# A convolution's first image: the table stored unnormalised, its scale and mean put back later

## The chip, the cores and the metric

The kernel runs on one core of one Trainium2 chip. The metric is the time of the device in microseconds for one execution. The engines are called PE (TensorE), DVE (VectorE), ACT (ScalarE), POOL (GpSimd) and SP (SyncE).

## The reference

The input `x` has 4 images of 256 channels and 64 x 64 positions. Layer 0 is a deformable convolution of the normalised images, added to `x`; layer 1 is an attention between the images and a mixture of experts. The change lies in layer 0 alone, and there in the first image alone:

```python
def _gn(v, G=32, eps=1e-5):            # mean and variance over 8 channels and all positions
    g = v.reshape(B_, G, C_ // G, H_, W_)
    ...
    return ((g - m) / jnp.sqrt(s + eps)).reshape(v.shape)

om = conv(x, w_off) + b_off            # x is the normalised image; 27 values a position
off = om[:, :2 * K2]                   # offsets of the 9 taps
mask = sigmoid(om[:, 2 * K2:])         # one factor for each tap and position
...
sampled = bilinear(x, ys, xs)          # 4 corners, weighted; outside the image: 0
sampled = sampled * mask
out = einsum('bckhw,ock->bohw', sampled, w_conv)
```

## The kernel before

An image is held channel by channel: two halves (`NCH` = 2, index `ch`) of 128 channels on the partitions, 4096 positions along them. Eight blocks (`NBLK`, index `q`) of 512 positions (`BLK`) make an image, and four groups (`NT`, index `i`) of 128 positions make a block.

**The opening** prepares the first image before any gather. SP issues the load of the image in four pieces (`load_piece`, L363), then the weights of the offsets (`woff_sb`, L376), `boff_sb` (L382), the weights of the convolution (`wconv_sb`, L394) and the zeros around the table (`borders`, L404 to L408). DVE takes the statistics of each piece as it comes (`stats`, L446); a small chain over PE, DVE and POOL gives for each channel the group's mean `gm`, the scale `rs` and the shift `nb` = -`gm` x `rs` (`group_of` to `shift`, L452 to L475). Then each block is normalised on DVE (`norm`, L508), turned by PE so that positions lie on the partitions (`turn`, L517), copied out of PSUM by ACT, and for the last group by DVE (`leave`, L530), and stored to the table in DRAM by four DMAs (L536). A row of the table holds the 256 channels of a position and those of the position below it; two rows, one after the other, are the four corners of a bilinear sample. The tiles that a turned block is collected in are `gs`, the ten buffers (`NGB`) that the gathers use afterwards. After that the offsets of the first two blocks (`EARLY`) are made: six products a block into `po` (`rows_of`, L548), three shifted copies by ACT into `oc` (L560), sums over the taps (`summed`, L569), and from them the indices and weights (`positions`, L626 to L648).

**The loop** then makes 288 steps (`STEPS`) for each image, one for every 128 positions and tap `k`. In iteration `n`: POOL gathers four corners for a later step (`gather`, L748; a buffer is used again when DVE has read its last corner); ACT weighs the first corner (`corner0`, L772, four steps ahead); DVE adds the other three (`corner`, L781); PE turns the sum back to channels (`turned`, L795) into one of three PSUM buffers of `ps_tp`; ACT copies the turned tile of the step before to `sT` (`to_sbuf`, L803); and PE makes one of the four products of an earlier tap (`product`, L815), which add up over the taps in `acc`. Work for the next image (load, statistics, table, offsets) and the offsets of the first image's other blocks are strung into the same loop at written-out steps: `later.append((step, fn))`.

The order on PE, DVE, ACT and POOL is the written one, in the opening (`emit(first)`, without POOL) as in the loop; an instruction that waits holds up all that follow it on its engine. SP issues its DMAs in the order in which they are written, or when their data are ready.

Of the kernel before, what the change touches and what calls it, by code (L numbers as in the profile page):

```python
# [9 lines left out]
F32 = mybir.dt.float32  # L10
I32 = mybir.dt.int32
AF = mybir.ActivationFunctionType
ALU = mybir.AluOpType
# [4 lines left out]
P = 128  # L18
B, C, H, W = 4, 256, 64, 64
HW = H * W  # L20
NCH = C // P
K2 = 9
NR = HW // P
NOFF = 3 * K2
QUAD = 32
# [10 lines left out]
BLK = 512  # L36
NT = BLK // P
RB = BLK // W


STEPS = NR * K2
# [4 lines left out]
OUT = 6  # L46
EARLIEST = 12
FIRST = 32
LOADS = (8, 18, 28, 38)
LANDED = 7  # L50
FIRST_HALF, SECOND_HALF = 189, 58
# [4 lines left out]
NBLK = HW // BLK  # L56
# [46 lines left out]
def conv_attn_moe_kernel(  # L103
# [229 lines left out]
    with ExitStack() as actx:  # L333
# [6 lines left out]


        azt = made.enter_context(tc.tile_pool(name="a_zt", bufs=2, side="right"))
        apad = made.enter_context(tc.tile_pool(name="a_pad", bufs=2, side="right"))
        atmp = made.enter_context(tc.tile_pool(name="a_tmp", bufs=1, side="right"))
        axs = [
# [14 lines left out]
        def load_piece(b, n):  # L360
            ch, h = divmod(n, 2)
            cols = slice(h * HW // 2, (h + 1) * HW // 2)
            return nc.sync.dma_start(  # L363
                xraw[b][:, ch, cols],
                x[b, ch * P : (ch + 1) * P].rearrange("p h w -> p (h w)")[:, cols],
            )

        image_tile(0)
        for n in range(2 * NCH):
            load_piece(0, n)  # L370


        woff_sb = aw.tile([P, NCH, 3, 3, QUAD], F32, name="woff_sb")
        V.memset(woff_sb, 0.0)
        for ch in range(NCH):
            nc.sync.dma_start(  # L376
# [9 lines left out]
            V.tensor_copy(tap_sum[ps], ident[ps, kj * QUAD : kj * QUAD + NOFF])  # L386


        ocs = [aw.tile([3 * QUAD, RB, W], F32, name=f"oc{n}") for n in range(3)]
# [3 lines left out]
        for ch in range(NCH):  # L393
            nc.sync.dma_start(wconv_sb[:, ch], w_conv[ch * P : (ch + 1) * P])  # L394
        rwc_sb = load_router(aw, "rwc_sb")


        zeros = aw.tile([P, C], F32, name="zeros")
        G.memset(zeros, 0.0)

        def borders(b):
# [6 lines left out]
            nc.sync.dma_start(  # L408
                tables[b].rearrange("(y x) (two c) -> y (x two) c", x=TW, two=2)[
                    : H + 1, 2 * (W + 1) :  # L410
                ],
                zv[: H + 1].to_broadcast([H + 1, 4, C]),
            )


        grid = aw.tile([P, 2, NR, K2], F32, name="grid")
# [14 lines left out]
        def pieces(b):  # L431
# [28 lines left out]
            def shift():  # L460
                V.scalar_tensor_tensor(nb, gm, -1.0, rs, ALU.mult, ALU.mult)

            n = FIRST
            out_ = later if b else first
            for ch in range(NCH):
                for j in range(NBLK):
                    at = LOADS[2 * ch + 2 * j // NBLK] + LANDED + j % (NBLK // 2)
                    out_.append((at if b else n, lambda ch=ch, j=j: stats(ch, j)))
                    n += 1
# [10 lines left out]
            xrv = xr.rearrange("p ch (h w) -> p ch h w", w=W)  # L480
            tv = tables[b].rearrange("(y x) (two c) -> y x two c", x=TW, two=2)
            oms = []

            def block(q, at, table=True, offsets=True, alone=False):

# [35 lines left out]

                def leave(i):
                    if i == 0:

                        t["zt"] = (
                            gs[q].rearrange("p (t c) -> p t c", c=C) if alone
                            else azt.tile([P, NT, C], F32, name=f"zt{b}_{q}", tag="zt")
                        )
                    zt = t["zt"]
                    (V.tensor_copy if alone and i == NT - 1 else S.copy)(zt[:, i, :], t["tp"])  # L530
                    if i < NT - 1:
                        return
                    for yl in range(2):
                        for two in range(2):
                            yy = q * RB + yl + 1 - two
                            stores[b] = nc.sync.dma_start(  # L536
                                tv[yy : yy + RB - 1 : 2, 1 : W + 1, two, :].rearrange(
                                    "t x c -> x t c"
                                ),
                                zt[yl * W : (yl + 1) * W],  # L540
                            )


                def rows_of(n):
# [6 lines left out]
                        start=(n == 0), stop=(n == NCH * 3 - 1),  # L551
                    )

                oc = ocs[q % 2 if table else 2]

                def shifted(kj):
                    ps = slice(kj * QUAD, (kj + 1) * QUAD)
# [6 lines left out]
                def summed(half):  # L564
# [3 lines left out]
                    for i in range(half * 2, half * 2 + 2):  # L568
# [2 lines left out]
                            start=True, stop=True,  # L571
                        )

                def kept():
                    if b and not q:
                        oms.append(atmp.tile([P, NR, NOFF], F32, name=f"om{b}", tag="om"))
                    of[q] = oms[0][:, rows_in(q), :] if b else atmp.tile(
                        [P, NT, NOFF], F32, name=f"om{b}_{q}", tag="om_", bufs=2
                    )
                    V.tensor_copy(of[q], t["pt"])  # L580

                out_.append((at, lambda: norm(0)))
                out_.append((at + 1, lambda: norm(1)))
                if alone and table:
                    for i in range(NT):
                        out_.append((at + 10 + 2 * i, lambda i=i: turn(i)))
                        out_.append((at + 11 + 2 * i, lambda i=i: leave(i)))
                elif table:
                    for i in range(NT):
                        out_.append((at + 3 + 4 * i, lambda i=i: turn(i)))  # L590
                        out_.append((at + 4 + 4 * i, lambda i=i: leave(i)))
                if offsets:
                    for m in range(NCH * 3):
                        out_.append((at + 4 + 2 * m + m // 2, lambda m=m: rows_of(m)))
                    for kj in range(3):
                        out_.append((at + 18 + kj, lambda kj=kj: shifted(kj)))
                    out_.append((at + 22, lambda: summed(0)))
                    out_.append((at + 23, lambda: summed(1)))
                    out_.append((at + 24, kept))
                return out_  # L600

            of = {}
# [105 lines left out]


            place_for()  # L710
            for q in range(NBLK):
                first.extend(block(q, n + 10 * q, offsets=False, alone=True))
            n += 10 * NBLK + 8
            for q in range(EARLY):
                at = n + 20 * q
                first.extend(block(q, at, table=False, alone=True))
# [82 lines left out]
        def to_sbuf(n):  # L799
            tap, i = divmod(n, NT)  # L800
            if i == 0:
                sTs[tap] = asm.tile([P, NCH, BLK], F32, name=f"sT{tap}", tag="sT", bufs=2)
            S.copy(  # L803
                sTs[tap][:, :, i * P : (i + 1) * P],
                tps.pop(n).rearrange("p (ch t) -> p ch t", ch=NCH),
            )

        def product(n):

            tap, part = divmod(n, NT)  # L810
            block, k = divmod(tap, K2)
            oh, ch = divmod(part, NCH)
            if k == 0 and ch == 0:
                accs[block, oh] = ps_acc.tile([P, BLK], F32, name=f"acc{block}_{oh}", tag="acc")
            T.matmul(  # L815
                accs[block, oh], wconv_sb[:, ch, k, oh * P : (oh + 1) * P], sTs[tap][:, ch, :],
                start=(k == 0 and ch == 0), stop=(k == K2 - 1 and ch == NCH - 1),
            )
            if part == NT - 1:
                del sTs[tap]  # L820

# [1331 lines left out]
```

## Time and profile before

| | us |
|---|---|
| median of 3 runs | 2981.97 (2981.52 to 2986.56) |
| the profiled execution | 2980.43 |
| its span in the profile | 2978.6 |
| first gather issued | 62.70 |
| PE busy over the span | 2808.4 (94%) |
| DVE, ACT, POOL busy | 2460.5 (83%), 1897.9 (64%), 1767.1 (59%) |

The shares of busy time are averages over stages with different limits. What matters here is the opening, up to the first gather, and the loop over the first image, up to about 510 us. A matmul's duration in a row includes the filling of the array; the distance from one start to the next is what it costs where PE is full. "x2" in a timeline counts instructions that stand side by side.

### The profile page before, as it was taken

To read this page: it belongs to the slowest core of one execution; us is meant where nothing else is said; L and a number is where in the kernel's file an instruction comes from. 1 tells how busy PE (TensorE), PEld (TensorE's weight loads), DVE (VectorE), ACT (ScalarE), POOL (GpSimd) and SP (SyncE) were. 2 spreads that over 40 slices of the span, in tenths; PEclk is the share of its full clock that TensorE was granted. 3 is DMA by queue.
4 is the path that set the end of the run, shared out by engine and by line. 5 is a ranking of instruction groups with operands and counts; after the bars stand their busy time and mean duration, and the time that the engine had idled before them with its cause. 6 is when DMAs were issued, how large, how long until landed. Compare 5 with 4: busy or idle time off the path is not lost. (4 is left out here: it accounts for less than half of the span.)

```text
span 2978.6 us, 46093 instructions
## 1 busy us (share of the span) xinstructions
PE 2808.4 (94%) x11356; PEld 1650.3 (55%) x11356; DVE 2460.5 (83%) x6413; ACT 1897.9 (64%) x4462; POOL 1767.1 (59%) x1809
## 2 busy tenths in 40 slices
PE   3899999899998899999999999999999999999997
PEld 2355554345554455544444444545555688888885
DVE  4988889998999999999999996987778785446777
ACT  2566665566765566755776664764876666666675
POOL 2665556666666676667777663320777677774442
PEclk8999999999999999999999999999999999999998
DMA  8999999999999999999999986961555556647988
GB/s 256 409 352 368 350 350 403 406 389 399 410 391 401 406 393 400 402 393 389 408 395 382 383 339 139 177 108 55 189 176 197 184 171 195 207 146 248 339 278 280
DMA packets 348551, 913.03 MB, mean 307 GB/s; under 512 B 42566, under 2 KB 125821, under 8 KB 345984
## 3 DMA queue, kind: packets, MB, share of 16 engines
q0 software_dynamic: 208368, 689.10, 62.5%
q1 hardware_dynamic: 129488, 197.93, 20.9%
q10 hardware_dynamic: 10432, 23.07, 2.1%
q8 instruction: 95, 1.56, 0.2%
q14 instruction: 168, 1.38, 0.1%
HBM read 741.09 MB, written 171.60 MB: 306 GB/s over the span
## 5 line engine op out<-in xcount | busy, mean ns | idle before, releaser
L748 POOL DMA_INDIRECT g<-table,idx x1152 | 1119.2, 971 | 611.7 <-DVE s L781 526.5
L815 PE MATMUL acc<-sT,wconv_sb 128*128 128x512 f32 x2304 | 1186.8, 597 | 22.3 <-ACT sT L803 18.8
L772 ACT ACTIVATE s<-g,wts 128x256 f32<-128x256 f32 x1152 | 587.0, 510 | 316.0 <-DMA g<-table,idx 241.3
L781 DVE SCALAR_TENSOR_TENSOR partial<-g,wts,s 128x256 f32<-128x256 f32 x1152 | 565.3, 491 | 124.2 <-ACT s L772 48.0
L795 PEld LDWEIGHTS tps<-ident,s 128*128 128x128 f32 x2304 | 295.3, 147 | 659.6 <-issue 275.1
L781 DVE SCALAR_TENSOR_TENSOR s<-g,wts,s 128x256 f32<-128x256 f32 x1152 | 550.1, 478 | 0.0
L803 ACT COPY sT<-tps 128x256 f32<-128x256 f32 x1152 | 417.8, 363 | 204.9 <-PE acc L815 113.6
L781 DVE SCALAR_TENSOR_TENSOR s<-g,wts,partial 128x256 f32<-128x256 f32 x1152 | 545.2, 473 | 0.7
L795 PE MATMUL tps<-ident,s 128*128 128x128 f32 x2304 | 458.6, 281 | 84.9 <-DVE s L781 43.7
L1935 POOL DMA_INDIRECT ys_rows<-y,to x277 | 276.0, 996 | 221.6 <-DVE y L1930 162.8
L815 PEld LDWEIGHTS acc<-sT,wconv_sb 128*128 128x128 f32 x2304 | 349.4, 192 | 33.2 <-ACT sT L803 30.5
L1508 POOL DMA_INDIRECT xs_rows<-u,slots x256 | 253.4, 990 | 95.0 <-issue 69.7
L1907 PE MATMUL ph<-xT,w 128*128 128x256 f32 (+1 forms) x1288 | 268.6, 351 | 7.4 <-ACT hT L1911 4.5
L1925 PE MATMUL py<-w,hT 128*128 128x256 f32 x1108 | 266.5, 380 | 0.6 <-ACT w L1874 0.6
L1930 DVE TENSOR_TENSOR y<-py,w 128x512 f32<-128x512 f32 (+1 forms) x161 | 99.3, 617 | 188.0 <-ACT w L1868 94.0
L1907 PEld LDWEIGHTS ph<-xT,w 128*128 128x128 f32 x1288 | 210.9, 191 | 28.6 <-ACT hT L1911 6.9
L1925 PEld LDWEIGHTS py<-w,hT 128*128 128x128 f32 x1108 | 206.9, 190 | 27.4 <-ACT w L1874 1.0
L1911 ACT ACTIVATE hT<-ph,w 128x256 f32<-128x256 f32 (+1 forms) x322 | 136.8, 443 | 129.1 <-PE ph L1907 127.5
L322 DVE SCALAR_TENSOR_TENSOR junk<-q,k 128x512 f32<-128x512 f32 x224 | 141.6, 686 | 20.6 <-ACT k L1107 20.5
L548 PE MATMUL po<-xs,woff_sb 128*96 128x512 f32 x288 | 147.2, 593 | 0.0
L1290 DVE SCALAR_TENSOR_TENSOR mix<-pv,att,mix 128x512 f32<-128x512 f32 x192 | 132.6, 742 | 6.8 <-PE pv L1026 2.8
L1874 ACT COPY w<-early_state 128x768 f32 x161 | 132.8, 825 | 0.0
(291 smaller groups left out, 3434.5 us busy)
## 6 DMA issues: line engine op xcount, KB each, us to landing
xt<-xs_rows SPq DMA_DIRECT2D x116, 260.0 KB
yk<-ys_rows SPq DMA_DIRECT2D x56, 512.0 KB
table<-zt SPq DMA_DIRECT2D x96, 256.0 KB
g<-table,idx POOLq DMA_INDIRECT x1152, 7.7
t<-o SPq DMA_DIRECT2D x32, 530.0 KB
t<-bo_sb POOLq DMA_DIRECT2D x32, 530.0 KB, 15.2
dt<-t SPq DMA_DIRECT2D x64, 265.0 KB
xraw<-in_x SPq DMA_DIRECT2D x16, 1024.0 KB
```

The lines of the kernel that those rows point to most:

```text
L322: V.scalar_tensor_tensor(junk, qks[s_, j, ch][0], 1.0, qks[t_, j, ch][1], ALU.mult, ALU.mult, accum_out=parts[:, ch, s_ * B + t_, j : j + 1],)
L548: T.matmul(t["po"], woff_sb[:, ch, ki].rearrange("p kj o -> p (kj o)"), t["xs"][:, ch, ki : ki + RB], start=(n == 0), stop=(n == NCH * 3 - 1),
L748: g = G.indirect_dma_start(out=gs[n % NGB], out_offset=None, in_=tables[b], in_offset=bass.IndirectOffsetOnAxis(ap=params[b][0][:, r, k : ...
L772: first = S.activation(ss[n], gs[n % NGB][:, :C], AF.Copy, scale=params[b][1][:, 0, r, k : k + 1])
L781: last_corner[n] = V.scalar_tensor_tensor(kept if c == 1 else ss[n], gs[n % NGB][:, c * C : (c + 1) * C], params[b][1][:, c, r, k : k + 1] ...
L795: T.transpose(tps[n][:, ch * P : (ch + 1) * P], s[:, ch * P : (ch + 1) * P], ident)
L803: S.copy(sTs[tap][:, :, i * P : (i + 1) * P], tps.pop(n).rearrange("p (ch t) -> p ch t", ch=NCH),)
L815: T.matmul(accs[block, oh], wconv_sb[:, ch, k, oh * P : (oh + 1) * P], sTs[tap][:, ch, :], start=(k == 0 and ch == 0), stop=(k == K2 - 1 a ...
L1508: s = G.indirect_dma_start(out=rows_, out_offset=bass.IndirectOffsetOnAxis(ap=slots[:, k, n : n + 1], axis=0), in_=u[:, n % NT, :], in_off ...
L1907: T.matmul(ph, w1_sb[:, ch, f * P : (f + 1) * P], xT[:, ch, :], start=(ch == 0), stop=(ch == NCH - 1),)
L1925: T.matmul(py[:, i, :], hT[:, f, i * P : (i + 1) * P], w2_sb[:, f, :], start=(f == 0), stop=(f == NCH - 1),)
L1935: s = G.indirect_dma_start(out=ys_rows[g], out_offset=bass.IndirectOffsetOnAxis(ap=to[:, i : i + 1], axis=0), in_=y[:, i, :], in_offset=No ...
```

## The change

Only the first image is treated differently. Its groups of 128 positions are turned straight from the loaded image (`raw`), as soon as the first halves of both channel halves are there, and stored without scale and mean; for that the four pieces of the load are issued in another order. The first 24 groups (`RAW`) come before the chain of the statistics on PE and ACT, the other 8 after it. As a place outside the image must count as zero after the normalisation, the border of the table now holds the mean of each channel (`mean_row`), so its stores come after the statistics; and the loads of `wconv_sb` and `rwc_sb` come after all stores of the table.

In the loop, the scale of each channel is applied where the turned tile is copied to `sT`: two ACTIVATEs of 128x128 with a scale for each partition take the place of one copy of 128x256. The mean is taken out by a product: `centre` (9 x 256) is the shift `nb` multiplied into the convolution's weights, made by `centre_part` at steps 1 to 5 of the loop, and each block's `acc` gets one more product for each half of its output, of `centre` with the masks of the nine taps. These are made by `turned_mask`, one product and one sigmoid for each block. The tile `spare`, in which the mean's row and `centre` are put together, takes the place that the second image is loaded to.

```diff
         image_tile(0)
-        for n in range(2 * NCH):
-            load_piece(0, n)
+        for h in range(2):
+            for ch in range(NCH):
+                load_piece(0, 2 * ch + h)
...
+            def raw(q, i):
+                zt = gs[q].rearrange("p (t c) -> p t c", c=C)
+                tp = ps_tp.tile([P, C], F32, name=f"tpx{b}_{q}_{i}", tag="tp")
+                for ch in range(NCH):
+                    T.transpose(
+                        tp[:, ch * P : (ch + 1) * P],
+                        xr[:, ch, q * BLK + i * P : q * BLK + (i + 1) * P], ident,
+                    )
+                S.copy(zt[:, i, :], tp)
+                if i == NT - 1:
+                    stored(q, zt)
+
+            def mean_row():
+                scale_of[b] = rs
+                pr = ps_om.tile([P, C], F32, name="mean_row", tag="om")
+                for ch in range(NCH):
+                    d = spare[:, 0, ch * P : (ch + 1) * P]
+                    V.tensor_scalar(d, ident, gm[:, ch : ch + 1], None, ALU.mult)
+                    T.matmul(pr[:, ch * P : (ch + 1) * P], ones, d, start=True, stop=True)
+                row = spare[:, 0, C : 2 * C]
+                S.copy(row, pr)
+                borders(b, row)
+
+            def centre_part(m):
+                ks = slice(2 * m, min(2 * m + 2, K2))
+                size = (ks.stop - ks.start) * C
+                pc = ps_tp.tile([1, BLK], F32, name=f"pc{m}", tag="tp")
+                for ch in range(NCH):
+                    T.matmul(
+                        pc[:, :size], nb[:, ch : ch + 1],
+                        wconv_sb[:, ch, ks].rearrange("p k o -> p (k o)"),
+                        start=(ch == 0), stop=(ch == NCH - 1),
+                    )
+                S.copy(spare[:1, 1, 2 * m * C : 2 * m * C + size], pc[:, :size])
+                if ks.stop == K2:
+                    nc.sync.dma_start(
+                        centre, spare[:1, 1, : K2 * C].rearrange("p (k o) -> p k o", o=C)
+                    )
...
-                oc = ocs[q % 2 if table else 2]
+                oc = ocs[0 if table else 1]
...
+                def turned_mask():
+                    pk = ps_tp.tile([K2, BLK], F32, name=f"pk{q}", tag="tp")
+                    T.matmul(
+                        pk, tap_sum[:, 2 * K2 :], oc.rearrange("p y x -> p (y x)"),
+                        start=True, stop=True,
+                    )
+                    masks[q] = asm.tile([K2, BLK], F32, name=f"mT{q}", tag="mT", bufs=2)
+                    S.activation(masks[q], pk, AF.Sigmoid)
...
                     out_.append((at + 24, kept))
+                    if not b:
+                        out_.append((at + 24, turned_mask))
...
-            for q in range(NBLK):
-                first.extend(block(q, n + 10 * q, offsets=False, alone=True))
-            n += 10 * NBLK + 8
+            for m in range(NBLK * NT):
+                q, i = divmod(m, NT)
+                at = 2 * q // NBLK if m < RAW else n + (m - RAW) / 2
+                first.append((at, lambda q=q, i=i: raw(q, i)))
+            first.append((n, mean_row))
+            n += 8
+            for m in range((K2 + 1) // 2):
+                later.append((1 + m, lambda m=m: centre_part(m)))
...
-            S.copy(
-                sTs[tap][:, :, i * P : (i + 1) * P],
-                tps.pop(n).rearrange("p (ch t) -> p ch t", ch=NCH),
-            )
+            tp = tps.pop(n).rearrange("p (ch t) -> p ch t", ch=NCH)
+            to = sTs[tap][:, :, i * P : (i + 1) * P]
+            if n >= STEPS:
+                S.copy(to, tp)
+                return
+            for ch in range(NCH):
+                S.activation(
+                    to[:, ch], tp[:, ch], AF.Copy, scale=scale_of[0][:, ch : ch + 1]
+                )
...
+            if block < NBLK and k == 1 and ch == 1:
+                T.matmul(
+                    accs[block, oh], centre[:, oh * P : (oh + 1) * P], masks[block],
+                    start=False, stop=False,
+                )
...
-        borders(0)
         todo = {}
         for when, fn in pieces(0):
             todo.setdefault(when, []).append(fn)
+        for ch in range(NCH):
+            nc.sync.dma_start(wconv_sb[:, ch], w_conv[ch * P : (ch + 1) * P])
+        rwc_sb = load_router(aw, "rwc_sb")
```

Left out are tiles moved to other pools, `stored` (the four stores of a block, unchanged, now a function) and the branches of `leave` and `block` that only the first image's table used.

More of the change, by code (lines that the diff above doesn't have):

```diff
@@ L48 @@
 FIRST = 32
+RAW = 24
 LOADS = (8, 18, 28, 38)
@@ L342, in conv_attn_moe_kernel @@
         azt = made.enter_context(tc.tile_pool(name="a_zt", bufs=2, side="right"))
+        amade = made.enter_context(tc.tile_pool(name="a_made", bufs=1, side="right"))
         apad = made.enter_context(tc.tile_pool(name="a_pad", bufs=2, side="right"))
@@ L368, in conv_attn_moe_kernel @@
         image_tile(0)
-        for n in range(2 * NCH):
-            load_piece(0, n)
-        woff_sb = aw.tile([P, NCH, 3, 3, QUAD], F32, name="woff_sb")
+        for h in range(2):
+            for ch in range(NCH):
+                load_piece(0, 2 * ch + h)
+        woff_sb = amade.tile([P, NCH, 3, 3, QUAD], F32, name="woff_sb")
         V.memset(woff_sb, 0.0)
@@ L386, in conv_attn_moe_kernel @@
             V.tensor_copy(tap_sum[ps], ident[ps, kj * QUAD : kj * QUAD + NOFF])
-        ocs = [aw.tile([3 * QUAD, RB, W], F32, name=f"oc{n}") for n in range(3)]
+        ocs = [amade.tile([3 * QUAD, RB, W], F32, name=f"oc{n}") for n in range(2)]
         for oc in ocs:
@@ L392, in conv_attn_moe_kernel, with borders @@
         wconv_sb = aw.tile([P, NCH, K2, C], F32, name="wconv_sb")
[L393 to L398, printed above, removed]
+        centre = aw.tile([K2, C], F32, name="centre")
+        spare = axs[1].tile([P, NCH, HW], F32, name="spare", tag="xraw")
+        masks, scale_of = {}, {}
+        zeros = amade.tile([P, C], F32, name="zeros")
         G.memset(zeros, 0.0)
-        def borders(b):
+        def borders(b, zeros=zeros):
             tv = tables[b].rearrange("(y x) (two c) -> y x two c", x=TW, two=2)
@@ L413, in borders @@
             )
-        grid = aw.tile([P, 2, NR, K2], F32, name="grid")
+        grid = amade.tile([P, 2, NR, K2], F32, name="grid")
         gi = atmp.tile([P, 2, NR, K2], I32, name="gi", tag="ki32")
@@ L461, in shift @@
                 V.scalar_tensor_tensor(nb, gm, -1.0, rs, ALU.mult, ALU.mult)
-            n = FIRST
+            n = FIRST + NCH * NBLK
             out_ = later if b else first
@@ L466, in pieces @@
                 for j in range(NBLK):
-                    at = LOADS[2 * ch + 2 * j // NBLK] + LANDED + j % (NBLK // 2)
-                    out_.append((at if b else n, lambda ch=ch, j=j: stats(ch, j)))
-                    n += 1
+                    h = 2 * j // NBLK
+                    at = LOADS[2 * ch + h] + LANDED + j % (NBLK // 2) if b else h
+                    out_.append((at, lambda ch=ch, j=j: stats(ch, j)))
             out_.append((n + 1, lambda: group_of(mv[:, :, 0])))
@@ L482, in pieces, with stored @@
             oms = []
+            def stored(q, zt):
+                for yl in range(2):
+                    for two in range(2):
+                        yy = q * RB + yl + 1 - two
+                        stores[b] = nc.sync.dma_start(
+                            tv[yy : yy + RB - 1 : 2, 1 : W + 1, two, :].rearrange(
+                                "t x c -> x t c"
+                            ),
+                            zt[yl * W : (yl + 1) * W],
+                        )
[35 more added lines that the diff above has]
+                    )
             def block(q, at, table=True, offsets=True, alone=False):
@@ L523, in leave @@
                     if i == 0:
-                        t["zt"] = (
-                            gs[q].rearrange("p (t c) -> p t c", c=C) if alone
-                            else azt.tile([P, NT, C], F32, name=f"zt{b}_{q}", tag="zt")
-                        )
[L529 to L541, printed above, removed]
+                        t["zt"] = azt.tile([P, NT, C], F32, name=f"zt{b}_{q}", tag="zt")
+                    S.copy(t["zt"][:, i, :], t["tp"])
+                    if i == NT - 1:
+                        stored(q, t["zt"])
                 def rows_of(n):
@@ L583, in block @@
                 out_.append((at + 1, lambda: norm(1)))
[L584 to L588, printed above, removed]
+                if table:
                     for i in range(NT):
@@ L802, in to_sbuf @@
                 sTs[tap] = asm.tile([P, NCH, BLK], F32, name=f"sT{tap}", tag="sT", bufs=2)
-            S.copy(
-                sTs[tap][:, :, i * P : (i + 1) * P],
-                tps.pop(n).rearrange("p (ch t) -> p ch t", ch=NCH),
-            )
+            tp = tps.pop(n).rearrange("p (ch t) -> p ch t", ch=NCH)
[7 more added lines that the diff above has]
+                )
         def product(n):
@@ L818, in product @@
             )
+            if block < NBLK and k == 1 and ch == 1:
+                T.matmul(
+                    accs[block, oh], centre[:, oh * P : (oh + 1) * P], masks[block],
+                    start=False, stop=False,
+                )
             if part == NT - 1:
```

## The prediction

> **What bounds the kernel now.** I read the page first, then busy time by stretches, because the page's shares average over stages. The chain of waits reaches back only to 2069 us and says nothing about the first image, where the whole edit lies. Columns below: busy microseconds and instruction count of each engine, granted clock, DMA share, rate.
>
> ```profile
> core 0: us, PE busy (x) PEld busy (x) DVE busy (x) ACT busy (x) POOL busy (x), PEclk, DMA share, GB/s
> 66.00:116.00 50.00, 35.74 (x111) 16.27 (x112) 41.63 (x97) 24.91 (x61) 36.65 (x37) 0.82 1.00 395
> 116.00:160.00 44.00, 38.58 (x150) 19.16 (x149) 42.51 (x114) 26.47 (x65) 24.56 (x28) 0.96 0.98 379
> 160.00:460.00 300.00, 296.68 (x1181) 157.34 (x1180) 255.88 (x675) 202.43 (x488) 175.76 (x188) 1.00 0.97 359
> 460.00:530.00 70.00, 62.80 (x227) 28.48 (x226) 65.20 (x154) 39.65 (x104) 47.51 (x51) 1.00 1.02 402
> ```
>
> The first image has four stretches. Up to 116 the gathers set the pace (395 GB/s), then DVE does (42.5 of 44), then from 160 to 460 PE does (296.7 of 300, while DMA falls to 359 GB/s and POOL waits), and at the end DMA again. A busy PE need not be at its peak, so I checked it with the groups of 210 to 460:
>
> ```profile
> L815 PE MATMUL acc<-sT,wconv_sb 128*128 128x512 f32 x308 | 157.7, 594 | 0.0
> L795 PE MATMUL tps<-ident,s 128*128 128x128 f32 x308 | 60.1, 277 | 1.6 <-DVE s L781 1.4 <-ACT sT L803 0.3
> L548 PE MATMUL po<-xs,woff_sb 128*96 128x512 f32 x82 | 42.0, 593 | 0.0
> ```
>
> and the time from one start to the next, in the timeline of PE:
>
> ```profile
> 302.68 0.38 PE L795 MATMUL tps<-ident,s 128*128 128x128 f32 x2
> 302.90 1.02 PE L815 MATMUL acc<-sT,wconv_sb 128*128 128x512 f32 x2
> 303.76 0.38 PE L795 MATMUL tps<-ident,s 128*128 128x128 f32 x2
> 303.98 1.02 PE L815 MATMUL acc<-sT,wconv_sb 128*128 128x512 f32 x2
> ```
>
> One product of the code is two MATMUL records ("x2"): an f32 product over 512 columns is two passes, and it takes 303.76 - 302.90 = 0.86 us, 0.43 a pass; a transpose takes 0.11. The stretch of 250 us holds 308 + 82 + 48 (`po` from tiles of other names) = 438 passes: 188 us; 398 transposes (`tps`, `tpx`, `back`): 44; 160 small passes of `pt` and `back` at about 0.1: 16. That is 248 of 250 us, so PE is full, and work added there costs its full time.
>
> The opening, in the timeline of SyncE and of POOL:
>
> ```profile
> 10.40 3.00 SPq L382 DMA_DIRECT2D boff_sb<-in_b_off  x1
> 13.45 0.82 SPq L394 DMA_DIRECT2D wconv_sb<-in_w_conv  x2
> 22.62 0.68 SPq L408 DMA_DIRECT2D table<-zeros  x1
> 24.00 34.55 SPq L536 DMA_DIRECT2D table<-g  x32
> 62.70 1.24 POOL L748 DMA_INDIRECT g<-table,idx  x1 [30.37 <-DMA beta_c<-in_beta]
> ```
>
> The 32 stores of the table run without a gap for 34.55 us; the first gather comes 4.1 us after the last issue. The gather needs every lane of the stores, so it is released by the last of them landing, though the label names a small load next to it. The indices of the second block were ready at 56.4 and do not hold it.
>
> **The change part by part.**
>
> *The stores start earlier.* The transposes no longer wait for the statistics, only for the two first halves (2.1 MB, by the bytes moved there at about 8.4 us). A turned group of 128 positions takes some 0.41 us (copies at L530), so block 0 stands at 10.3 us and later blocks every 1.7 us, faster than their four stores go out (4 x 1.08). SyncE is free when `boff_sb` is issued: 13.45. The 32 stores still take 34.55 us. The five border stores, which went out from 14.9 to 23.3 beside `wconv_sb`, now stand in that queue: 652 KB against 256 KB in 1.08 us is 2.75 us (bounds: 0 if they fit in, 8.4 as their issues took before). So the last issue ends at 13.45 + 34.55 + 2.75 = 50.75 and the first gather starts at 54.9: **7.8 us earlier** (2.2 to 10.6). Indices: 24 groups by some 18.2 us, the chain's 3.1, the mean's row and 8 more groups put PE's last raw transpose at about 25.3 instead of 33.3 us, so the second block's indices, at 56.4 before, follow near 48: not late. The 16 DVE normalisations and 8 DVE copies that go away lay before that and are covered.
>
> *The ramp.* `wconv_sb` (2.36 MB, 5.9 us at 400 GB/s) is moved behind the stores. It starts as the last stores land, so part falls in the 4.3 us in which the first gather has not landed yet. Then at steps 1 to 5 `centre_part` puts two products each on PE, in order behind the turned tiles, while the granted clock is still 0.50 (windows of 70 to 80) and a product takes about 1.9 us (80.32 to 82.19 in the timeline), then 0.86. ACT stands behind each: the copy of `pc` waits for PE, and the next `s` is queued after it; DVE and the gathers wait for `s`. Followed through the old times of these steps, with three `ps_tp` buffers, `s` of step 10 is 8.5 us late; the gathers hold 4 us in hand there (gather 10 issues at 75.7, its buffer was free at 71.6). At step 8 the second image's load waits for `centre` to leave the spare tile, and DVE's statistics of step 15 queue behind that load. None of these is seen in the trace; bounds 0 and 12 us, I take **5**, near the 4.5 us by which 8.5 exceeds the slack, with little for `wconv_sb`.
>
> *PE in the loop.* Each block gets two products with `centre` and one for `masks`, each over 512 columns; nine contracted rows do not shorten it, since it is the columns that move. In the PE-bound stretch (iterations 55 to 240 by the count of `acc`) fall the centre products of blocks 2 to 6 and the masks of blocks 3 to 7: 10 + 5 = 15, at 0.86 us: **12.9 us**. The other 7 (4 + 1 before 160, 2 after 460) lie where DVE or DMA ends last; were they on the path too, 18.9. The lower bound is 6, if waits that the busy time hides take half.
>
> The Trainium skill, TensorE: Matmul & The Clock Gate (section "Wait — 56ns, not 53.3ns?"), gives 215.7 ns from start to start for 512 columns on a warm array. By that, one pass a product, the 15 would be 3.2 us and the total near 3 us slower, no change that can be measured; the trace has 0.86 us at granted clock 1.00, and that is used.
>
> *ACT in the loop.* `to_sbuf` becomes two ACTIVATEs of 128x128 for a COPY of 128x256. An ACTIVATE of 128x128 from PSUM takes 367 ns (L1911). Neighbours overlap: an `s` of 0.51 us at 300.14 is followed at 300.55, a COPY of 0.37 us at 307.48 at 307.75, so by 0.10 us, and one of 128 occupies 0.26. So does the COPY now. So +0.26 us a step, 75 us over 288 steps, on an engine that is 67% busy. Only bursts are over the top. I added 0.26 for each step to ACT's busy time in slices of 5 us from 66 to 531: 19 of 93 slices exceed 5 us, by 10.3 us in all (those from 301 to 316 hold `oc` copies), and most can pass their excess on to the next, idler slice. With 1.5 us allowed for that, 0.9 stays. The masks' sigmoids add 0.7 us six times, mostly next to those bursts. I take **3**, from 1 to 12.
>
> The Trainium skill, ScalarE: Activation LUTs (section "What ACT_TABLE_LOAD costs"), speaks against this edit more strongly: an ACTIVATE with a pointer operand costs 280 ns plus 0.833 ns per element and neighbours overlap by 93 ns. Estimated from that, two of 128 occupy 0.59 us, so ACT's addition would be 0.33 us a step instead of 0.26; the sum does not use it.
>
> *Without effect:* one `oc` buffer fewer (its last reader is four steps after the writer, the next writer a period of 22 later), pools moved, the order of the four image pieces.
>
> *Sum:* -7.8 + 5 + 12.9 + 3 = +13.1 us on the profiled execution's own 2980.43 us: 2993.5. The median of the runs shown is 1.5 us above that execution, so 2995.0. About 0.2% (6 us) is what a measurement of this kernel can tell from no change. The later images and stages follow in order, so nothing is absorbed after the first image.
>
> **The rivals.**
>
> *Faster: PE has room after all.* Decided between 160 and 460: if PE's 296.7 us hide stalls that the 22 products can fill, and the ramp is absorbed by the gathers' slack, the earlier stores alone are left: 2982.0 - 7.8 = 2974. For it: POOL waits there for DVE, not for PE by name. Against: passes and transposes add up to 248 of 250 us. It turns faster once loop and ramp together cost under 2 us. 0.14.
>
> *Nearly even.* Ramp and bursts are absorbed, PE pays: -7.8 + 12.9 = 5, 2987. Within what can be told. 0.18.
>
> *ACT becomes the bound.* The bursts' 10.3 us and more are paid in full, PE waits for `sT`, and the ramp costs its 12: -7.8 + 12 + 12.9 + 12 = +29, 3011. For it: ACT ran without a gap from 299.9 to 312.4. Against: 98 of 300 us idle. 0.13.
>
> *The gathers do not start earlier.* Something else behind the stores holds the first gather (borders at their old price, `wconv_sb` sharing the rings): the gain shrinks to 0 and the rest stays: +21, 3003. 0.05.
>
> **How the numbers follow.** The forecast as summed has 0.50. Its own range, by the terms' nearer bounds, is 2988 to 3003. The 0.18 case reaches down to 2981, the ACT case to 3011; I take 2979 to 3011, which leaves out most of the faster case and the upper half of the ACT case, 0.13 and 0.06. Faster by over 0.2%: 0.14; within: the even case, 0.18; slower: the rest, 0.68.
>
> **What would show it.** In the changed profile: the first store issued near 13.5, the first gather near 55; pieces of `pc` on PE around 65 to 75 and a hole in the gathers after them; between the first gather and the second image's steps, some 13 to 20 us more than before; 30 passes of `centre` and `pk` in the PE-bound stretch at 0.43 apart, and PE still full there; ACT 80% busy. Wrong if the first image's loop is no longer than before (PE was not full), or if ACT has no idle time and PE waits for `sT` (price too low).

## The result and the profile after

| | before | after |
|---|---|---|
| median of 6 runs each, same chip, us | 2984.98 (2981.52 to 2988.17) | 3010.32 (3007.12 to 3012.5) |
| ratio to before, 95% interval | | 1.0086 [1.0076, 1.0097] |
| profiled execution, us | 2980.43 | 3008.6 |
| its span, us | 2978.6 | 3006.8 |
| first gather issued, us | 62.70 | 58.58 |
| from gather 80 to gather 248 of the first image, us | 277.2 | 297.7 |

The kernel became slower by 25 us, twice the 13 that the sum gave. First the stretches of the kernel after (columns as in the prediction; the third now ends at 480):

```profile
66.00:116.00 50.00, 44.72 (x135) 16.96 (x136) 40.09 (x93) 33.31 (x95) 30.73 (x33) 0.90 1.02 398
116.00:160.00 44.00, 39.06 (x146) 17.91 (x145) 42.27 (x114) 30.16 (x86) 23.60 (x26) 0.96 0.95 358
160.00:480.00 320.00, 315.57 (x1211) 159.73 (x1210) 256.45 (x674) 247.39 (x679) 175.41 (x188) 1.00 0.94 338
480.00:552.00 72.00, 67.78 (x239) 29.51 (x238) 67.39 (x159) 53.26 (x160) 48.70 (x52) 1.00 1.01 391
```

PE is as full as before (315.6 of 320 us), but DVE does the work of about 300 us in 320 (256.45, before 255.88 in 300) and the transfers fall from 359 to 338 GB/s. ACT rises from 67 to 77%, not to its limit. So the shape is the forecast one: PE sets the pace and was given more to do.

What it was given shows in the timeline of PE, four products and transposes that follow one another:

```profile
335.70 1.02 PE L875 MATMUL acc<-sT,wconv_sb 128*128 128x512 f32 x2
336.66 1.12 PE L880 MATMUL acc<-mT,centre 9*128 9x512 f32 x2
337.71 0.44 PE L850 MATMUL tps<-ident,s 128*128 128x128 f32 x2
337.98 1.02 PE L875 MATMUL acc<-sT,wconv_sb 128*128 128x512 f32 x2
```

The centre product (L880) takes 337.71 - 336.66 = 1.05 us. The product ahead of it takes 0.96 instead of 0.86 and the transpose behind it 0.27 instead of 0.22. Together that is 1.2 us where the prediction had 0.86.

The opening, in the timeline of SyncE:

```profile
13.42 25.25 SPq L491 DMA_DIRECT2D table<-g  x24
38.77 1.09 SPq L407 DMA_DIRECT2D table<-spare  x1
39.91 1.06 SPq L408 DMA_DIRECT2D table<-spare  x1
41.01 0.78 SPq L409 DMA_DIRECT2D table<-spare  x1
41.83 1.65 SPq L410 DMA_DIRECT2D table<-spare  x1
43.53 0.46 SPq L411 DMA_DIRECT2D table<-spare  x1
44.09 9.97 SPq L491 DMA_DIRECT2D table<-g  x8
54.11 2.31 SPq L1025 DMA_DIRECT2D wconv_sb<-in_w_conv  x2
```

The first store goes out at 13.42, as forecast. But the five border stores hold the queue for 5.3 us (38.77 to 44.09), and the eight stores behind them take 1.25 us each instead of 1.08. The last issue ends at 54.06 instead of the 50.75 of the prediction, and the first gather follows 4.5 us later. So it is not the bytes that take this time: between two stretches of this kernel (columns as above), the first with stores of blocks, the second with those of the border, the DMA share falls from 0.88 to 0.50 and the rate from 248 to 140 GB/s.

```profile
24.00:38.80 14.80, 12.63 (x27) 5.03 (x26) 3.03 (x17) 4.34 (x7) 0.00 (x0) 0.74 0.88 248
38.80:44.10 5.30, 3.45 (x9) 1.00 (x7) 0.00 (x0) 1.70 (x3) 0.00 (x0) 1.00 0.50 140
```

Where the time arises can be read from the gathers. The table gives by how many microseconds gather n of the first kernel named is later than gather n of the kernel before (its first profile); the other columns are experiments from below, on a chip of the same speed.

| gather | after | before, repeated | without the load of `wconv_sb` | borders first, 128 rows | bare loop |
|---|---|---|---|---|---|
| 0 | -4.1 | 0.2 | -4.0 | -3.9 | -4.0 |
| 16 | -3.9 | 0.1 | -4.4 | -3.7 | -4.1 |
| 20 | -1.0 | -0.1 | -3.2 | -0.8 | -1.3 |
| 30 | 2.3 | 0.6 | 0.9 | 2.6 | 2.2 |
| 65 | 1.8 | 0.5 | 0.4 | 2.2 | 1.8 |
| 80 | 2.1 | 0.5 | 0.7 | 2.2 | 1.8 |
| 248 | 22.6 | 0.5 | 21.1 | 18.6 | 1.6 |
| 1148 | 21.8 | 1.7 | 21.3 | 17.8 | 3.1 |

The lead of 4.1 us is lost between gathers 16 and 30; from gather 80 to 248 another 20.5 us are lost, spread over the stretch; of these 0.8 us come back in three more images.

### The profile page after: what moved, and what is told of

The parts are those of the page before. It is cut to its first block, busy times and chain, and to the rows that moved or that the text cites. A ratio compares the mean times of both kernels' runs of the same rounds, so it can differ in the third digit from the quotient of the medians.

```text
span 3006.8 us, 46517 instructions
## 1 busy us (share of the span) xinstructions
PE 2850.1 (95%) x11428; PEld 1659.0 (55%) x11428; DVE 2450.7 (82%) x6390; ACT 1973.6 (66%) x4772; POOL 1769.4 (59%) x1809
## 5 line engine op out<-in xcount | busy, mean ns | idle before, releaser
L875 PE MATMUL acc<-sT,wconv_sb 128*128 128x512 f32 x2304 | 1184.6, 596 | 17.4 <-ACT sT L861 13.4
L861 ACT COPY sT<-tps 128x256 f32<-128x256 f32 x864 | 312.7, 362 | 134.8 <-PE acc L875 80.9
L864 ACT ACTIVATE sT<-tps,rs 128x128 f32<-128x128 f32 x576 | 179.0, 364 | 65.1 <-PE acc L875 35.1
L323 DVE SCALAR_TENSOR_TENSOR junk<-q,k 128x512 f32<-128x512 f32 x224 | 141.7, 687 | 21.8 <-ACT k L1174 21.7
## 6 DMA issues: line engine op xcount, KB each, us to landing
table<-zt SPq DMA_DIRECT2D x96, 256.0 KB, 12.1
```

Source lines behind the costliest of these rows:

```text
L861: S.copy(to, tp)
L864: S.activation(to[:, ch], tp[:, ch], AF.Copy, scale=scale_of[0][:, ch : ch + 1])
L875: T.matmul(accs[block, oh], wconv_sb[:, ch, k, oh * P : (oh + 1) * P], sTs[tap][:, ch, :], start=(k == 0 and ch == 0), stop=(k == K2 - 1 a ...
```

## The experiments

The first two sets ran on chips on which the kernel before itself took 3372.4 and 3319.3 us, the third on one with 2986.3 us; so only ratios of one set and the first image's stretches are compared.

### First set: each part alone

**One copy.** The scale is left out of the loop.

```diff
-            if n >= STEPS:
-                S.copy(to, tp)
-                return
-            for ch in range(NCH):
-                S.activation(
-                    to[:, ch], tp[:, ch], AF.Copy, scale=scale_of[0][:, ch : ch + 1]
-                )
+            S.copy(to, tp)
```

> The changed kernel with one COPY of 128x256 to sT in the first image too, so without the scale of each channel (its time is read as the change less the split copy). PE theory (the loop's growth is the 22 extra products on a full PE): 2 to 4 us less than the changed kernel, so 21 to 23 us over before, and the gathers of steps 80 to 250 still fall back by 16 us or more. ACT theory (the growth is the split copy): 15 to 20 us less, so 5 to 10 us over before, and the gathers of steps 80 to 250 fall back by under 6 us.

**No products.** The mean is left in: no masks and no products with `centre`.

```diff
-                    if not b:
-                        out_.append((at + 24, turned_mask))
...
-            if block < NBLK and k == 1 and ch == 1:
-                T.matmul(accs[block, oh], centre[:, oh * P : (oh + 1) * P], masks[block], ...)
```

> The changed kernel without the products with centre and without the masks' product and sigmoid (the mean stays in; centre is still made at steps 1 to 5, the copies are still split). PE theory: the gathers of steps 80 to 250 fall back by 2 to 4 us only, and the time is 16 to 19 us under the changed kernel, so 6 to 9 us over before. ACT theory: still 14 us or more of falling back in the loop, and at most 6 us under the changed kernel.

**No parts.** `centre` is zero from the start, and steps 1 to 5 have no pieces.

```diff
+        G.memset(centre, 0.0)
...
-            for m in range((K2 + 1) // 2):
-                later.append((1 + m, lambda m=m: centre_part(m)))
```

> The changed kernel without the ten products and five copies of steps 1 to 5 (centre is filled with zeros on POOL, its DMA is left out; the products with it in the loop stay). If these hold up ACT and the gathers in the ramp: the lead of 4 us at the first gather stays to step 30, and the time is 5 to 7 us under the changed kernel, so 18 to 20 us over before. Rival (the weights of the convolution, loaded late, and the second image's load cost the ramp): the gathers between steps 15 and 30 still fall back by 4 us or more, and the time is within 2 us of the changed kernel.

**Two copies.** The kernel before, with the split copy put into its first image, at a scale of one.

```diff
-            S.copy(sTs[tap][:, :, i * P : (i + 1) * P], tps.pop(n).rearrange(...))
...
+            for ch in range(NCH):
+                S.activation(to[:, ch], tp[:, ch], AF.Copy, scale=ones[:, ch : ch + 1])
```

> The kernel before with the first image's COPY to sT split in two ACTIVATEs of 128x128 with a scale for each partition (a column of ones), and nothing else. PE theory: 1 to 4 us over before, all of it in steps 80 to 250. ACT theory: 12 us or more over before.

| | ratio to before | gather 0 | gather 80 to 248 |
|---|---|---|---|
| one copy | 1.0029 [1.0004, 1.0054] | 58.94 | 297.2 |
| no products | 1.0019 [0.9998, 1.0041] | 59.10 | 295.4 |
| no parts | 1.0047 [1.0026, 1.0068] | 58.78 | 301.1 |
| two copies | 1.0018 [0.9998, 1.0038] | 63.38 | 290.5 |

This set did not settle much. The intervals overlap, and the whole kernel after was not among the runs, so the four could only be set beside a profile from a faster chip. That neither part alone brings the stretch back to 277 looked as if each cost 13 to 20 us. Time and stretch even spoke for opposite theories: one copy is 9.9 us over before, as the ACT theory had it, with a stretch as long as the PE theory had it; with no products it is the other way round (7.2 us over before, a stretch 18 us above 277).

### Second set: the same with the kernel after beside them

> The changed kernel itself, to stand beside the next three on one chip. 0.7 to 1.0% over before; its gathers gain 4 us at the first, lose 5 to 6 us between steps 16 and 30 and some 20 us between steps 80 and 250.

> The changed kernel without the products with centre and the masks' products and sigmoids in the loop, beside the changed kernel on one chip. PE theory: 16 to 19 us under the changed kernel, of which 16 or more between steps 80 and 250. ACT theory: at most 6 us under it.

> The changed kernel with one COPY to sT in place of the two scaled ACTIVATEs (the scale of each channel is left out), beside the changed kernel on one chip. PE theory: 1 to 4 us under it. ACT theory: 12 us or more under it, all between steps 80 and 250.

> The changed kernel without the making of centre at steps 1 to 5 (centre is zeros; the products with it stay), beside the changed kernel on one chip. Ramp theory (the copies of pc keep ACT from the first corners): the gathers fall back by under 1.5 us between steps 10 and 30, and the time is 4 to 7 us under the changed kernel. Rival (late weights, late second image): they still fall back by 4 us or more there, and the time is within 2 us of it.

| | ratio to before | gather 20 | gather 30 | gather 80 to 248 |
|---|---|---|---|---|
| after | 1.0056 [1.0035, 1.0078] | 90.33 | 107.10 | 298.4 |
| no products | 1.0013 [0.9995, 1.0030] | 92.38 | 108.57 | 289.4 |
| one copy | 1.0020 [1.0003, 1.0037] | 92.55 | 107.83 | 293.9 |
| no parts | 1.0051 [1.0036, 1.0067] | 84.98 | 107.27 | 297.4 |

Taking the products out shortens the stretch by 9.0 us, taking the split copy out by 4.5; neither alone nor added do they make 20.5, nor do they fit either theory. By the medians the two runs are 14.7 and 15.1 us under the kernel after; what exceeds the stretches arises in the later images (from gather 248 to 1148 they take 1444 and 1432 us, the kernel after 1450), although their code is the same. So on this chip the stretches are compared, not the times. It seems that something else holds the stretch on these chips. In the later images, which are the same in all these kernels, the stretch of 1000 to 1300 reads, for the kernel before on the first chip:

```profile
1000.00:1300.00 300.00, 293.95 (x1180) 155.38 (x1179) 276.00 (x674) 203.65 (x507) 197.98 (x207) 0.99 1.02 399
```

and for the kernel after in this set:

```profile
1000.00:1300.00 300.00, 266.16 (x1002) 132.98 (x1001) 254.97 (x613) 169.64 (x435) 180.16 (x188) 0.97 0.97 364
```

So this chip moves about 364 GB/s where the first moves 399, and the first image's loop at its old pace needs 359. A loop freed of the products may run into the transfers: the run without products moves 341 GB/s there. By this reading the two sets give only lower bounds for what the parts cost. But on average 359 would still fit. And the gathers of that run wait 25.9 us (190 to 460) for nothing that the profile shows, against 2.6 in the kernel before on the faster chip; those of the kernel after wait 25.3 on the slower chip as well, so this wait goes with the chip and says nothing of the products. The next set ran on a faster chip, so for the slower ones the reading is argued, not shown.

Without the pieces of `centre`, gather 20 comes 5.3 us earlier, which is the predicted mechanism; but by gather 30 all of it is gone again, and the time is 3.5 us under the kernel after, within the noise of both. The waits of that run from 83 to 103 us name no cause for the largest single ones (each line: what waits and for what, the sum in us, the number of waits, the longest):

```profile
POOL g L802 <- DVE s L835: 10.3, 7, 2.8
...
DVE partial L835 <- ACT s L826: 5.1, 4, 2.5
PEld acc L874 <- issue: 4.6, 1, 4.6
ACT sT L863 <- remote: 4.6, 2, 4.0
PE acc L874 <- issue: 4.4, 1, 4.4
DVE partial L835 <- issue: 3.3, 1, 3.3
```

The run with two copies, whose opening is that of the kernel before and which has no pieces, shows such holes too: ACT waits for `remote` 9.4 us in two of them, and from gather 20 to gather 30 it takes 20.0 us, against 13.4 in the kernel before on the faster chip. No run on the faster chips shows a wait for `remote` there. So what the pieces cost on a chip without these holes is not told by this run.

### Third set: floor, closure and two prices

**The kernel before, repeated**, as the floor of its chip.

> The kernel before, unchanged, profiled on this chip as the floor of the first image's loop. In the first pair its stretch from gather 80 to gather 248 was 277.2 us, the changed kernel's 297.7; without the loop's products it was 289.4, with one copy 293.9, on chips on which later images ran slower. If those chips hold this stretch back too (transfers), this run gives 286 to 290 there, and the edit's price in the loop is only about 10 us on such a chip, the products 9 and the copies the rest. If the stretch is PE's on every chip, it gives 276 to 279, the edit costs 20, and products (9) and copies (4.5) leave 6 us unexplained. From gather 0 to gather 30: 40 us if the opening's transfers are the same (before 40.0, after 46.5 and 48.8).

Ratio 0.9995 [0.9986, 1.0005]; the stretch 277.2 us, gather 0 to 30 40.5 us. It is the floor of the first pair again, so this chip compares with that pair.

**Without the load of `wconv_sb`**, whose place is filled with a constant.

```diff
+        G.memset(wconv_sb, 0.02)
...
-            for ch in range(NCH):
-                nc.sync.dma_start(wconv_sb[:, ch], w_conv[ch * P : (ch + 1) * P])
```

> The changed kernel without the load of the convolution's weights (they are filled with a constant instead, so the result lacks them). From gather 0 to gather 30 the kernel before took 40.0 us, the changed one 46.5 and 48.8. Theory (the load of 2.36 MB, which in the kernel before lay in a hole of the transfers ahead of the stores, now stands among gathers that keep the transfers full, and costs its bytes: 2.36 MB at 0.41 MB/us = 5.8 us): 40 to 43 us here, and the time falls by about 5 us against the changed kernel of the last call, ratio near 1.004 or below. Rival (the pieces of the centre rows and the later load of the second image do it, as predicted): 46 to 49 us, and the time is unchanged. First gather at 58.3 to 58.6 in both.

Ratio 1.0071 [1.0058, 1.0084]; gather 0 to 30 takes 44.9 us, neither 40 to 43 nor 46 to 49. The load costs about 1.5 us of the ramp, not 5.8: this theory of mine falls. The stalls stay. They are these, in POOL's timeline of the kernel after:

```profile
78.25 0.94 POOL L803 DMA_INDIRECT g<-table,idx  x1 [0.31 <-issue]
79.95 0.94 POOL L803 DMA_INDIRECT g<-table,idx  x1 [0.76 <-DVE s L836]
82.48 0.93 POOL L803 DMA_INDIRECT g<-table,idx  x1 [1.60 <-DVE s L836]
85.03 0.94 POOL L803 DMA_INDIRECT g<-table,idx  x1 [1.61 <-DVE s L836]
87.00 0.94 POOL L803 DMA_INDIRECT g<-table,idx  x1 [1.03 <-DVE s L836]
...
99.72 0.94 POOL L803 DMA_INDIRECT g<-table,idx  x1 [2.25 <-DVE s L836]
```

The first group, from 79.95 to 87.00, ends a chain that ACT's timeline shows: each copy of a piece waits a microsecond for PE, and the next `s` stands behind it.

```profile
77.78 0.57 ACT L534 COPY spare<-pc 1x512 f32<-1x512 f32 x1 [1.16 <-PE pc L529]
78.26 0.50 ACT L827 ACTIVATE s<-g,wts 128x256 f32<-128x256 f32 x1
78.67 0.59 ACT L864 ACTIVATE sT<-tps,rs 128x128 f32<-128x128 f32 x2
80.32 0.57 ACT L534 COPY spare<-pc 1x512 f32<-1x512 f32 x1 [1.06 <-PE pc L529]
```

The second, at 99.72, is DVE's statistics of the second image, which wait 1.3 us for its load; that load was issued at 90.63 instead of 81.39; it waits for the copy of `centre` out of the spare tile, which was issued at 85.43.

**Borders first, and 128 rows.** Two edits in separate stages: the border stores go ahead of the others, with zeros in place of the mean; `centre` and the masks are padded with zeros to 128 rows.

```diff
-        centre = aw.tile([K2, C], F32, name="centre")
+        centre = aw.tile([P, C], F32, name="centre")
+        G.memset(centre, 0.0)
+        padded = [aw.tile([P, BLK], F32, name=f"mT{i}") for i in range(2)]
+        for m in padded:
+            G.memset(m, 0.0)
...
-                borders(b, row)
...
-                    masks[q] = asm.tile([K2, BLK], F32, name=f"mT{q}", tag="mT", bufs=2)
-                    S.activation(masks[q], pk, AF.Sigmoid)
+                    masks[q] = padded[q % 2]
+                    S.activation(masks[q][:K2], pk, AF.Sigmoid)
...
+        borders(0)
```

> The changed kernel with two edits in separate stages: the five border stores go out ahead of the table's stores, with zeros (the border lacks the mean), and the centre rows and masks are padded with zeros from 9 rows to 128. Opening: by the prediction's price of the borders (2.75 us) the first gather comes at 55.6 to 55.9 instead of 58.3 to 58.6; if the five stores hold up the queue for their whole 5.3 us and stretch the last eight stores, which took 1.25 us each behind them instead of 1.08, at 52 to 54. If the borders now delay the first stores by as much instead, it stays near 58. Loop: in the changed kernel the product with 9 rows takes 1.15 to 1.2 us from its neighbour's start to the next; if the few rows cause the excess over 0.86 us, it is 0.85 to 0.9 here and the stretch from gather 80 to gather 248 falls by 3 to 5 us; if the cause is another (a switch of the accumulator, a wait on the masks), 1.15 to 1.2 stays and the stretch stays at 298.

Ratio 1.0067 [1.0053, 1.0081]. SyncE's timeline of this kernel, with the borders now at the head:

```profile
13.53 0.51 SPq L411 DMA_DIRECT2D table<-zeros  x1
...
17.27 0.54 SPq L415 DMA_DIRECT2D table<-zeros  x1
17.93 36.53 SPq L495 DMA_DIRECT2D table<-g  x32
54.50 2.19 SPq L1029 DMA_DIRECT2D wconv_sb<-in_w_conv  x2
```

The first gather stays at 58.80. The 37 stores take from 13.5 to 54.5 in this order and from 13.4 to 54.1 in the other: in both the issues follow one another almost without a gap, and the borders cost their 4.4 to 5.3 us wherever they stand. In the loop, PE's timeline:

```profile
333.88 1.02 PE L878 MATMUL acc<-sT,wconv_sb 128*128 128x512 f32 x2
334.74 1.02 PE L883 MATMUL acc<-mT,centre 128*128 128x512 f32 x2
335.60 0.38 PE L853 MATMUL tps<-ident,s 128*128 128x128 f32 x2
```

With 128 rows the same product takes 335.60 - 334.74 = 0.86 us, and its neighbours take their usual time. The stretch falls from 297.7 to 293.7 us.

**Bare loop.** The opening of the kernel after; in the loop neither products nor masks, and one copy without a scale.

> The changed kernel with its opening, but in the loop neither products with the centre rows, nor masks, nor the scale: one copy of 128x256 as in the kernel before (the result lacks scale and mean). If products and scaled copies are all that the loop pays, the stretch from gather 80 to gather 248 is that of the kernel before on this chip (277 to 279, or 286 to 290 if transfers hold it there), and the two singly measured parts (9 and 4.5 us) together fall short of or reach the difference. If the opening's order also costs in the loop (later indices, fewer buffers), it stays 3 us or more above the kernel before. Time: the start's gain of 4 us less the ramp's 6 and the centre pieces: ratio 1.000 to 1.001.

Ratio 1.0014 [1.0005, 1.0023]. The stretch is 277.1 us, the floor to a tenth, and its line is that of the kernel before, PE's busy time included:

```profile
160.00:460.00 300.00, 296.68 (x1183) 157.79 (x1182) 256.06 (x675) 202.11 (x490) 177.70 (x189) 1.00 0.97 358
```

So the whole 20.5 us of the loop are products, masks and split copies, and nothing of the opening reaches into it. It also shows that the ramp eats the earlier start without masks and split copies too: this kernel still has the pieces and the late loads, and at gather 65 it is 1.8 us behind, as the kernel after is.

## Why the prediction was right in sign and half in size

| step | predicted | measured in the traces |
|---|---|---|
| first gather | -7.8 | -4.1 |
| ramp, to gather 65 | +5 | +5.9 |
| PE in the loop, gathers 80 to 248 | +12.9 | +18.7 |
| ACT in the loop, the same stretch | +3 | +1.8 (the rest of 20.5) |
| the rest, up to the last gather | 0 | -0.5 |
| after the last gather | 0 | +6.4 in this execution |
| sum | +13.1 | +28.2 of span; the medians differ by 25.3 |

The measured 3010.32 lies 15 us above the sum and outside the sum's own range, 2988 to 3003. The stated range, up to 3011, holds it by 0.7 us only because the case in which ACT becomes the bound had been counted in, and that case did not come. This part of the agreement is luck.

**PE.** That PE is full and pays for every added product was right: the rival in which PE has room fell with the stretch of 297.7 us. The step that failed is the price, "nine contracted rows do not shorten it". They do not shorten it, they make it longer. Counted from start to start with the neighbours' excess, ten centre products took 12.1 us (1.21 each) and five for the masks 6.6 (1.12 three times, 1.35 once, and 1.85 once, of which 0.68 is a transpose waiting for the sigmoid to free a `ps_tp` buffer). The padded run gave 4.0 us of it back. Why few rows cost more, no run shows. The masks' products contract 96 rows and fill 9, and their neighbours are lengthened in the same way; no run changed those. The rule of the Trainium skill that the prediction weighed (TensorE: Matmul & The Clock Gate, "Wait — 56ns, not 53.3ns?", 215.7 ns for 512 columns), taken as one pass a product, would by estimate have priced the 15 at 3.2 us and the change at no difference. The measurement decides: the trace's two passes of 0.43 us were the right choice for f32.

**ACT.** The price of the split copy held, in ACT's timeline of the kernel after:

```profile
301.52 0.51 ACT L827 ACTIVATE s<-g,wts 128x256 f32<-128x256 f32 x1
301.92 0.62 ACT L864 ACTIVATE sT<-tps,rs 128x128 f32<-128x128 f32 x2
302.42 0.39 ACT L581 COPY zt<-tpx 128x256 f32<-128x256 f32 x1
```

Two of 128x128 occupy 302.42 - 301.92 = 0.50 us, as worked out from the rows (0.52), and less than the 0.59 estimated from the Trainium skill (ScalarE: Activation LUTs, "What ACT_TABLE_LOAD costs"). Most of it lay beside PE. What is left for it is 20.5 - 18.7 = 1.8 us, or 1.3 by the padded run (293.7 - 277.2 = 16.5; products 8.6 + 6.6). This is a remainder and no measurement: no run on a faster chip has the split copies alone, and PE's named waits for `sT` rise only from 1.2 to 2.2 us in the stretch. The rival "ACT becomes the bound" named 3011, nearly the time that came, and is wrong all the same: ACT had 73 of 320 us idle.

**The opening.** Two terms were mis-sized. The borders were priced by their bytes, 2.75 us, but take 5.3 us; and the eight stores behind them take 9.97 us instead of 8.64. The step that failed is that price by bytes: while the borders are issued the DMA engines are half idle. With the landing (4.5 instead of 4.1) and the first 24 stores (25.25 instead of 25.9) that is 2.55 + 1.33 + 0.4 - 0.65 = 3.6 of the missing 3.7 us. The indices were not late, as forecast.

**The ramp.** Its size was about right. The chain through PE, ACT and `s` is seen as predicted, and so is the later load of the second image. Masks and split copies have no part in it: the bare loop takes 46.2 us from gather 0 to gather 30, the kernel after 46.5, the kernel before 40.0. The load of `wconv_sb` is worth 1.5 us. What pieces and later load of the second image cost singly is not shown: the pieces were taken away on slower chips alone, and holes without a releaser stand there in the stretch in which the lead is lost.

**After the last gather** the profiled executions of all four changed kernels on the faster chips lose 5 to 7 us more, the kernel before repeated gains 1. No code there was changed. If each kernel's excess in the medians is taken in place of its one profiled execution, less its lag at the last gather, -0.6 to 3.5 us are left; the cause is open.

No version here is faster than the kernel before: the bare loop only reaches its pace, and the changed opening with its ramp does not gain. An opening without the pieces was not run on a faster chip.

## What to carry to other kernels

Before work is put on an engine, add up its passes from start to start in the stage where it will lie; if they fill the stage, everything added is paid, and a small operation is not a cheap one: price it by a row of its own shape, or from above. Stores that move within a queue whose issues already follow one another are not hidden but only reordered, and small ones cost more there than their bytes. And when parts are taken out one by one, run the floor on the same chip: on slower chips the same parts showed other prices.

## What the runs showed that was not expected

An f32 product over 512 columns with 9 contracted rows took 1.05 us from start to start, and 1.21 with what it added to its neighbours; padded with zeros to 128 rows it took 0.86. Padding made it cheaper by 0.35 us.

Chips differed by a tenth: the later images moved 399 GB/s on one and 364 on another, and the kernel before took 2985 and 3319 us (3372 on a third). The same change cost 0.86% on the first and 0.56% on the second.
